# Gated cross-attention with RMS norm on one core: the setup's weight loads, transposes and first product rearranged

## The chip, the cores and the metric

The kernel runs on one core of a Trainium2 chip. The metric is the device time in microseconds of one execution, start to end. The kernel before was run three times: 1008.8, 1011.82 and 1014.79 us, median 1011.82. A profile is one further execution with the hardware profiler on.

## What is computed

All tensors are float32. x is (8, 1024, 1024), the memory ctx is (8, 64, 512), W_mem is (1024, 512), W_gate is (1024, 2048), b_gate and norm_w have 1024 elements.

```
memory_proj    = ctx @ W_mem.T                             # (8, 64, 1024), "mp"
scores         = x @ memory_proj.T / sqrt(1024)            # (8, 1024, 64)
attn           = softmax(scores)
memory_context = attn @ memory_proj                        # (8, 1024, 1024)
gate           = sigmoid(concat(x, memory_context) @ W_gate.T + b_gate)
fused          = x + gate * memory_context
out            = fused * rsqrt(mean(fused**2) + 1e-6) * norm_w
```

W_gate falls into W1 (applied to x) and W2 (applied to memory_context). Since memory_context is attn @ mp, the kernel computes mp @ W2.T + b_gate once for all 512 memory rows ("G2") and applies attn to that; so only x @ W1.T is a large product. That one is done with Strassen-Winograd's seven products at two levels, hence the many sums and differences of quarters of x and of W1.

## The kernel before

The kernel is one long function with inner helpers. All of it is written out in program order (`pin` keeps each instruction in the order of the source, engine by engine). DMAs go out on SyncE's queue (helper `load`, L96), on ScalarE's queue (helper `scratch`, L99) and, for the residual, on GpSimd's. Dependences, and the completion semaphores of DMAs, are put in by the framework. TensorE's matmuls all come from the helper `mm` (L90), and two-operand sums from `tt` (L93), so in the profile they are told apart by their tiles.

Setup, L114 to L430:

- SyncE loads the memory (mem_sb, 4 DMAs of 128 rows), W_mem transposed (wm, 4 DMAs of 512 KB), the bias (broadcast to 128 partitions), the first half of the columns of W2 (w, 16 DMAs of 128 KB, runs of 2 KB), then W1 (ws, 32 DMAs of 128 KB, runs of 1 KB). Rows of W1 and W2 are loaded in quarters of 32 partitions (`rows_by_chunk`, L104), because the main loop transposes x in 32x32 blocks and the feature order must agree.
- TensorE transposes the memory through PSUM (pt_mem, L165), VectorE copies it out (memT, L171) and puts W_mem's columns into block order (wmp, L179).
- pm (L195 to L204): for each of eight blocks j of 128 features, four matmuls over the chunks k of the memory's 512 columns give mp transposed (mpT). ScalarE and VectorE copy the sums out by turns; pairs of blocks are stored to DRAM (mpd), from which the main loop loads each batch's part for the scores (mpb).
- TensorE transposes mpT back (pt_mp, L211), ScalarE copies it (L213) into `mp` and stores it to DRAM (mgd, L221), the rows that attn multiplies.
- pg (L400 to L428): eight sums n, for two halves h of W2's columns and four blocks q of 128 memory rows, each of eight 128x512 matmuls. VectorE adds the bias into a staging tile, ScalarE stores that to the other half of mgd. Between the adds VectorE works off `w1_tasks`: four large outer differences (128x2048) and 28 inner ones (128x512) of W1's blocks, which have a tile of their own for each of the seven outer products (`ws`, 7 slots each). After add 0 come the loads of W2's second half and of the first tile of x; after add 6 the block transposes of x, the first sums, and GpSimd's inner sums.

Main loop: sixteen tiles of 512 rows of x, seven outer products each, 49 products per tile. A table of due times (`plan`) puts loads, transposes, softmax, sums, sigmoid, residual and norm into fixed slots between the products. The first product of the first tile is kA of `outer_product` (L633).

The pools matter for the order: the xq pool has 4 buffers of 4 KB per partition (wm, then mp, then x), the gate pool 7 (W2, then the outputs), apool, rot and small one or two for each name; PSUM has five banks for sums in turn, two for the context and one for scores.

Of the kernel before, what the change touches and what calls it, by code (L numbers as in the profile page):

```python
# [8 lines left out]
F32 = mybir.dt.float32  # L9
AF = mybir.ActivationFunctionType  # L10
ALU = mybir.AluOpType
# [4 lines left out]
P = 128  # L16
# [4 lines left out]
def tile_gated_cross_attention_rmsnorm(  # L21
# [40 lines left out]
    nc = tc.nc  # L62
    B, N, D = x.shape
    M, E = mem.shape[1:]
# [3 lines left out]
    BM = B * M  # L68
    KD = D // P
    KE = E // P  # L70
    H = 512
    C = 256
    NPAIR = BM // P
# [15 lines left out]
    def mm(o, lhsT, rhs, start, stop):  # L89
        pin(nc.tensor.matmul(o, lhsT, rhs, start=start, stop=stop, skip_group_check=True))  # L90

    def tt(eng, o, a, b, op):
        pin(eng.tensor_tensor(o, a, b, op))  # L93

    def load(o, i):
        pin(nc.sync.dma_start(o, i))  # L96

    def scratch(o, i):
        pin(nc.scalar.dma_start(o, i))  # L99

    def t4k(pool, shape, tag, name):
        return pool.tile(shape, F32, tag=tag, name=name)
# [7 lines left out]
    def bank(n, shape, name):  # L110
        return ps.tile(shape, F32, tag=banks[n % 5], name=name)


    memr = mem.rearrange("b m e -> (b m) e").rearrange("(q p) e -> p q e", p=P)  # L114
    mem_sb = [t4k(rot, [P, 2, E], "l2", f"mem_sb{i}") for i in range(2)]
    for q in range(NPAIR):
        load(mem_sb[q // 2][:, q % 2, :], memr[:, q, :])
    wm = []
    for k in range(KE):
        t = t4k(xqpool, [P, D], "xq", f"wm{k}")  # L120
        load(t, w_mem_t[k * P : (k + 1) * P, :])
        wm.append(t)
    bias_sb = t4k(small, [P, D], "junk", "bias_sb")
    load(bias_sb, b_gate.partition_broadcast(P))
    w2r = rows_by_chunk(w_gate_t[D:, :])
    w2 = {}

    def load_w2(h):
        for k in range(KD // 2):
            t = t4k(gpool, [P, 2, H], "gate", f"w2_{k}_{h}")  # L130
            for i in range(4):
                load(
                    t[32 * i : 32 * (i + 1), :, :],
                    w2r[i][:, 2 * k : 2 * k + 2, h * H : (h + 1) * H],
                )
            w2[k, h] = t

    load_w2(0)

    w1r = rows_by_chunk(w_gate_t[:D, :])  # L140
    ws = {o: const.tile([P, 7, 2, C], F32, name=f"ws{o}") for o in range(1, 8)}
    R11, R21, R12, R22, T4, T1, T2 = range(7)
    for o, k, h in ((1, 0, 0), (7, 0, 1), (3, 1, 1), (2, 1, 0)):
        for i in range(4):
            for n in range(2):
                load(
                    ws[o][32 * i : 32 * (i + 1), 2 * n : 2 * n + 2, :, :],
                    w1r[i][:, 4 * k : 4 * k + 4, h * H + n * C : h * H + (n + 1) * C],
                )
    nw_sb = const.tile([P, D], F32, name="nw_sb")  # L150

    ident = const.tile([P, P], F32, name="ident")
# [3 lines left out]


    mpd = dram.tile([P, KD, BM], F32, name="mpd")
    mgd = dram.tile([B, 2, M, D], F32, name="mgd")
    memT = [t4k(apool, [P, 2, BM], f"a1{i + 1}", f"memT{i}") for i in range(2)]  # L160
    for q in range(NPAIR):
        pt = bank(q, [P, KE, P], f"pt_mem{q}")
        for k in range(KE):
            pin(
                nc.tensor.transpose(  # L165
                    pt[:, k, :], mem_sb[q // 2][:, q % 2, k * P : (k + 1) * P], ident
                )
            )
        for i in range(2):
            pin(  # L170
                nc.vector.tensor_copy(  # L171
                    memT[i][:, :, q * P : (q + 1) * P], pt[:, 2 * i : 2 * i + 2, :]
                )
            )
    wmp = []
    for k, tag in enumerate(("a21", "a22", "s1", "s2")):
        t = t4k(apool, [P, KD, P], tag, f"wmp{k}")
        pin(
            nc.vector.tensor_copy(  # L179
                t.rearrange("p j (i r) -> p j i r", r=32),  # L180
                wm[k].rearrange("p (i j r) -> p j i r", i=4, r=32),
            )
        )
        wmp.append(t)

    mpT = [
        t4k(rot, [P, 2, BM], tag, f"mpT_{tag}_{i}")
# [4 lines left out]
    def mp_rows(j, q):  # L192
        return mpT[j // 2][:, j % 2, q * P : (q + 1) * P]

    for j in range(KD):  # L195
        pm = bank(j, [P, BM], f"pm{j}")
        for k in range(KE):
            mm(pm, wmp[k][:, j, :], memT[k // 2][:, k % 2, :], k == 0, k == KE - 1)
        dst = mpT[j // 2][:, j % 2, :]
        if j % 2 == 0:  # L200
            pin(nc.scalar.copy(dst, pm))
        else:
            pin(nc.vector.tensor_copy(dst, pm))
            scratch(mpd[:, j - 1 : j + 1, :], mpT[j // 2])  # L204

    for q in range(NPAIR):
        stage = t4k(xqpool, [P, D], "xq", f"mp{q}")
        for h in range(2):
            pt = bank(2 * q + h, [P, 4, P], f"pt_mp{q}_{h}")
            for j in range(4):  # L210
                pin(nc.tensor.transpose(pt[:, j, :], mp_rows(4 * h + j, q), ident))  # L211
            pin(
                nc.scalar.copy(  # L213
                    stage.rearrange("p (i j r) -> p j i r", i=4, r=32)[
                        :, 4 * h : 4 * h + 4, :, :
                    ],
                    pt.rearrange("p j (i r) -> p j i r", r=32),
                )
            )
        for i in range(2):  # L220
            scratch(mgd[2 * q + i, 0], stage[i * M : (i + 1) * M, :])  # L221


    def outer_sum(o, a, b):
        tt(nc.vector, ws[o][:, 0:4, :, :], ws[a][:, 0:4, :, :], ws[b][:, 0:4, :, :], ALU.subtract)

    def inner_sums(o):
        w = ws[o]
        for s, a, b in ((T1, R12, R11), (T2, R22, T1), (R12, R22, R12), (T4, R21, T2)):
            yield lambda s=s, a=a, b=b: tt(  # L230
                nc.vector, w[:, s, :, :], w[:, a, :, :], w[:, b, :, :], ALU.subtract
            )


# [2 lines left out]
        *inner_sums(1),  # L237
        lambda: outer_sum(6, 3, 5),
        lambda: outer_sum(7, 3, 7),
        lambda: outer_sum(4, 2, 6),  # L240
    ] + [f for o in (6, 7, 5, 4, 2, 3) for f in inner_sums(o)]


    xq, A, S, L2, O = {}, {}, {}, {}, {}
# [59 lines left out]
    def inner_s(q, o, part):  # L304
        l11, l12, l21, l22 = quarters(left(q, o))
        if part == 0:
            L2[q, o] = t4k(rot, [P, 4, 2, P], "l2", f"l2_{q}_{o}")
        s1, s2, s3, s4 = (L2[q, o][:, i, :, :] for i in range(4))
        if part == 0:
            tt(nc.gpsimd, s1, l21, l22, ALU.add)  # L310
            tt(nc.gpsimd, s2, s1, l11, ALU.subtract)
        else:
            tt(nc.gpsimd, s3, l11, l21, ALU.subtract)
            tt(nc.gpsimd, s4, l12, s2, ALU.subtract)
# [71 lines left out]

    def load_mg(b):
        mgs[b] = t4k(small, [P, D], "mg", f"mg{b}")
        load(mgs[b], mgd[b].rearrange("g m d -> (g m) d"))


    first = [
# [7 lines left out]
    for h in range(2):  # L400
        cols = slice(h * H, (h + 1) * H)
        for q in range(NPAIR):
            pg = bank(n, [P, H], f"pg2_{h}_{q}")
            for k in range(KD):
                mm(pg, mp_rows(k, q), w2[k // 2, h][:, k % 2, :], k == 0, k == KD - 1)
            pool, tag = ((apool, "s4"), (small, "attnT"))[n % 2]
            stage = t4k(pool, [P, H], tag, f"g2_{h}_{q}")
            tt(nc.vector, stage, pg, bias_sb[:, cols], ALU.add)
            for i in range(2):
                scratch(mgd[2 * q + i, 1][:, cols], stage[i * M : (i + 1) * M, :])  # L410
            if n == 0:
                load_w2(1)
                for t in (0, 1, 2, 3):
                    load_xq(0, t)
                load(nw_sb, norm_w.partition_broadcast(P))
            if n < 6:
                while done < len(w1_tasks) * (n + 1) // 6:
                    w1_tasks[done]()
                    done += 1
            elif n == 6:  # L420
                for f in first:
                    f()
                for part in range(2):
                    inner_s(0, 1, part)
            n += 1
    load_mp(0)
    load_mg(0)
# [148 lines left out]
    def outer_product(q, o, ext):  # L576
# [1 line left out]
        nonlocal slot, banks  # L578
        l11, l12, l21, l22 = quarters(left(q, o))
        s1, s2, s3, s4 = (L2[q, o][:, i, :, :] for i in range(4))  # L580
        w = ws[o]
        kb = {}

        def product(name, tag, lhsT, s, start=True):
            nonlocal slot
            step()
            if name not in kb:
                kb[name] = ps.tile([P, C], F32, tag=banks[tag], name=f"k{name}{q}_{o}")
            for k in range(2):
                mm(kb[name], lhsT[:, k, :], w[:, s, k, :], start and k == 0, k == 1)  # L590
            slot += 1

        def o_blocks(row, h):
# [160 lines left out]
```

## Time and profile before

| What | Value |
|---|---|
| Three runs | 1008.8, 1011.82, 1014.79 us |
| Profiled execution | 1009.18 us, its span 1007.4 us |
| First product kA starts | 105.83 us into the span |
| pm on TensorE | 9.04 to 37.6 us |
| pg on TensorE | 44.56 to 105.8 us |
| A matmul of 128x512 | 0.43 us start to start |
| VectorE: 128x2048 difference, 128x512 difference, bias add | 2.29, 0.62, 0.69 us |
| SyncE: one DMA of 128 KB | issued in 0.35 to 0.47 us, landed after 2.4 us or more |
| HBM read and written | 85.98 and 39.85 MB |

How to read the lines below: "PE" is TensorE, "PEld" its weight loads, "DVE" VectorE, "ACT" ScalarE, "POOL" GpSimd, "SPq" and "ACTq" the DMA issues on the queues of SyncE and ScalarE. A line of the timeline has the start, the time taken, the engine, the source line, the operation, what it writes and reads by the program's tile names, the shape, how often, and in brackets how long the engine was idle before and what ended that. A line of stages has the stretch, its width, then busy time and count for PE, PEld, DVE, ACT and POOL, the granted TensorE clock, the share of DMA engines busy, and GB/s. A line of waits has who waited for whom, the total in us, the times, and the longest.

### The profile page before, as it was taken

Reading aid. Unit: us, or ns where it says so; the run is one execution under the profiler, and the core shown is the slowest. Engines: PE = TensorE matmul, PEld = TensorE weight load, DVE = VectorE, ACT = ScalarE, POOL = GpSimd, SP = SyncE. Lnnn points to the kernel's source line nnn. Section 1 sums busy time; section 2 is a strip of 40 time slices with the busy share of each in tenths; the row PEclk is TensorE's granted clock in tenths of the full one; section 3 lists DMA queues with packets and bytes.
Section 4 is the critical chain, followed back from the end, with each engine's and each line's share of the span. In section 5 each row is a group of like instructions: output and inputs, shape, how many; then the busy total and the mean of one; then the engine's idle time right before and its main releaser. Section 6 shows DMA issues by size and latency. Waiting matters only on the chain.

```text
span 1007.4 us, 14639 instructions
## 1 busy us (share of the span) xinstructions
PE 978.7 (97%) x4976; PEld 765.6 (76%) x4976; DVE 760.2 (75%) x1478; ACT 324.7 (32%) x600; POOL 688.0 (68%) x851
## 2 busy tenths in 40 slices
PE   7898999999999999999999999999999999999995
PEld 3443688888878887888888788878888887888883
DVE  2075667878878787878788787878787887878777
ACT  0200023334241523333342415233333424152344
POOL 0000577878878687878788786878787887868772
PEclk9999999999999999999999999999999999999998
DMA  8676508263633727182715546181826363372512
GB/s 255 198 182 180 135 1 178 84 138 97 157 101 84 188 78 164 63 185 87 163 60 130 141 104 158 52 199 63 178 83 137 96 167 97 84 188 89 142 63 84
DMA packets 76522, 126.79 MB, mean 126 GB/s; under 512 B 16288, under 2 KB 53152, under 8 KB 76448
## 3 DMA queue, kind: packets, MB, share of 16 engines
q1 hardware_dynamic: 65312, 88.11, 30.1%
q0 software_dynamic: 8640, 31.46, 17.0%
q10 hardware_dynamic: 2496, 6.29, 2.1%
q8 instruction: 39, 0.64, 0.3%
q14 instruction: 35, 0.29, 0.1%
HBM read 85.98 MB, written 39.85 MB: 125 GB/s over the span
## 4 chain that ended last, share of the span: by engine, by line
PE 79%; DVE 14%; DMA 3%; issue 2%; SPq 1%; ACT 1%; ACTq 0%; POOL 0%; DVEq 0%
PE kA L90 16%; PE pc L90 11%; PE kE L90 9%; PE kF L90 8%; PE kD L90 8%; PE kB L90 8%; PE kC L90 7%; PE psT L90 6%; DVE gate L520 4%; DVE gate L93 3%; PE pm L90 2%; PE pg L90 2%; DVE e L93 2%; DVE u L93 1%; DMA mgd<-g 1%
## 5 line engine op out<-in xcount | busy, mean ns | idle before, releaser
L93 POOL TENSOR_TENSOR gate<-gate,u 128x256 f32<-128x256 f32 x336 | 269.2, 831 | 122.3 <-DVE u L93 100.8
L93 POOL TENSOR_TENSOR l<-a 128x256 f32<-128x256 f32 x128 | 125.6, 981 | 163.3 <-DVE a L267 100.0
L491 ACT ACTIVATE gate<-gate 128x512 f32<-128x512 f32 x128 | 79.1, 629 | 397.7 <-DVE gate L93 397.6
L90 PE MATMUL kA<-ws,a 128*128 128x256 f32 x512 | 131.7, 380 | 0.4 <-ACT u L634 0.4
L90 PE MATMUL pc<-mg,attnT 64*128 64x256 f32 x512 | 127.4, 389 | 0.0
L520 DVE SCALAR_TENSOR_TENSOR gate<-gate,ss,nw_sb 128x512 f32<-128x512 f32 x120 | 116.5, 980 | 1.1
L90 PE MATMUL kC<-ws,l 128*128 128x256 f32 x448 | 115.1, 379 | 0.8 <-DVE g L93 0.8
L90 PE MATMUL kD<-ws,l 128*128 128x256 f32 x448 | 115.0, 379 | 0.0
L90 PE MATMUL kB<-ws,l 128*128 128x256 f32 x448 | 115.0, 379 | 0.0
L90 PE MATMUL kF<-ws,l 128*128 128x256 f32 x448 | 115.0, 379 | 0.0
L90 PEld LDWEIGHTS pc<-mg,attnT 64*128 64x128 f32 x512 | 90.6, 186 | 29.7 <-issue 21.2
L90 PEld LDWEIGHTS kA<-ws,a 128*128 128x128 f32 x512 | 97.0, 190 | 14.7 <-ACT u L634 1.2
L90 PE MATMUL kA<-ws,s 128*128 128x256 f32 x384 | 100.3, 384 | 1.1 <-ACT u L634 1.1
L90 PEld LDWEIGHTS kB<-ws,l 128*128 128x128 f32 x448 | 85.1, 190 | 11.6
L90 PEld LDWEIGHTS kF<-ws,l 128*128 128x128 f32 x448 | 85.1, 190 | 11.6
L90 PEld LDWEIGHTS kC<-ws,l 128*128 128x128 f32 x448 | 83.8, 190 | 11.8 <-POOL l L93 1.1
L90 PEld LDWEIGHTS kD<-ws,l 128*128 128x128 f32 x448 | 83.9, 190 | 10.7
L93 DVE TENSOR_TENSOR gate<-gate,pc 128x512 f32<-128x512 f32 x128 | 87.1, 680 | 5.5 <-ACT gate L491 5.5
L267 DVE STREAM_TRANSPOSE a<-xq 128x512 f32<-128x512 f32 x128 | 86.0, 693 | 0.0
L90 PEld LDWEIGHTS kA<-ws,s 128*128 128x128 f32 x384 | 71.6, 190 | 16.7 <-DVE a L93 6.2
L93 POOL TENSOR_TENSOR l<-s 128x256 f32<-128x256 f32 x96 | 77.9, 811 | 8.0 <-PE kF L90 5.4
L93 DVE TENSOR_TENSOR u<-u,kB 128x256 f32<-128x256 f32 x112 | 46.8, 418 | 46.2 <-PE kB L90 40.2
(94 smaller groups left out, 1695.4 us busy)
## 6 DMA issues: line engine op xcount, KB each, us to landing
xq<-in_x SPq DMA_DIRECT2D x256, 128.0 KB, 5.5
gate<-in_x POOLq DMA_DIRECT2D x60, 512.0 KB, 7.5
out<-gate SPq DMA_DIRECT2D x60, 512.0 KB, 2.6
w<-in_w_gate_t SPq DMA_DIRECT2D x32, 128.0 KB, 3.4
ws<-in_w_gate_t SPq DMA_DIRECT2D x32, 128.0 KB, 3.1
mg<-mgd SPq DMA_DIRECT2D x8, 512.0 KB, 3.6
wm<-in_w_mem_t SPq DMA_DIRECT2D x4, 512.0 KB, 6.4
mgd<-mp ACTq DMA_DIRECT2D x8, 256.0 KB, 4.4
```

Source lines behind the costliest of these rows:

```text
L90: pin(nc.tensor.matmul(o, lhsT, rhs, start=start, stop=stop, skip_group_check=True))
L93: pin(eng.tensor_tensor(o, a, b, op))
L267: nc.vector.transpose(A[key][:, :, r * P : (r + 1) * P].rearrange("p j (s c) -> p s j c", c=32), xq[q, t].rearrange("p s (j r) -> p s j r" ...
L491: pin(nc.scalar.activation(g, g, AF.Sigmoid))
L520: nc.vector.scalar_tensor_tensor(g[:, cols], g[:, cols], rstd[:, t % 2 : t % 2 + 1], nw_sb[:, cols], ALU.mult, ALU.mult,)
```

## The change

- Loads: the memory comes in eight DMAs of 128 KB (two halves of 256 rows, each in four quarters of the columns, runs of 512 B) into block layout `memq`, W_mem in sixteen DMAs of 32 whole rows; in the order first half of the memory, first chunk of W_mem, second half, other chunks. W2 comes as eight tiles of whole rows (32 DMAs of 32 rows of 4 KB), all ahead of W1; W1 as two tiles of whole rows (32 DMAs), no longer as quarters in the tiles `ws`. What used to be slots of `ws` is now a view of these tiles, of three tiles for outer differences, or a slot of a small tile `it` (`w_op`).
- Transposes: the memory and mp are transposed by VectorE in 32x32 blocks (4 and 16 instructions of 128x512), not by TensorE. The copies of the pm sums are all on VectorE.
- pm: the chunks k are the outer loop and the eight sums are open together in eight PSUM banks; the first chunk is done in two halves of the columns.
- Stores: mpd's four stores follow all eight copies in the source; mp's rows go to mgd in sixteen DMAs of 128 KB in place of eight of 256 KB; the bias adds' results in eight of 256 KB in place of sixteen.
- pg: as before, with whole-row tiles; the staging tiles are those of mg and attnT. The W1 differences are spread over five adds in place of six, in another order; the first tile's transposes follow adds 5 and 6.
- mg is loaded in two DMAs.

The diff, cut to its core:

```diff
-    memr = mem.rearrange("b m e -> (b m) e").rearrange("(q p) e -> p q e", p=P)
-    mem_sb = [t4k(rot, [P, 2, E], "l2", f"mem_sb{i}") for i in range(2)]
-    for q in range(NPAIR):
-        load(mem_sb[q // 2][:, q % 2, :], memr[:, q, :])
-    wm = []
-    for k in range(KE):
-        t = t4k(xqpool, [P, D], "xq", f"wm{k}")
-        load(t, w_mem_t[k * P : (k + 1) * P, :])
-        wm.append(t)
+    memq = [t4k(rot, [P, BM // 64, E // 4], "l2", f"memq{i}") for i in range(2)]
+    wm = [t4k(xqpool, [P, D], "xq", f"wm{k}") for k in range(KE)]
+    def load_mem(g):
+        for i in range(4):
+            load(memq[g][32 * i : 32 * (i + 1), :, :], memr[g, i])
+    def load_wm(k):
+        for i in range(4):
+            load(wm[k][32 * i : 32 * (i + 1), :], wmr[i, k])
+    load_mem(0)
+    load_wm(0)
+    load_mem(1)
+    for k in range(1, KE):
+        load_wm(k)
...
-    load_w2(0)
+    for k in range(KD):
+        t = t4k(*((gpool, [P, D], "gate") if k < 7 else (apool, [P, D], "s4")), f"w2_{k}")
+        for i in range(4):
+            load(t[32 * i : 32 * (i + 1), :], w2r[i][:, k, :])
+        w2.append(t)
...
+    w1 = [const.tile([P, 4, D], F32, name=f"w1_{h}") for h in range(2)]
+    for h in range(2):
+        for k in range(4):
             for i in range(4):
+                load(w1[h][32 * i : 32 * (i + 1), k, :], w1r[i][:, 4 * h + k, :])
...
+    def w_op(o, s):
+        if s >= T4:
+            return inner_t[o][:, s - T4, :, :]
+        k, n = {R11: (0, 0), R21: (1, 0), R12: (0, 1), R22: (1, 1)}[s]
+        return outer_b[o][:, 2 * k : 2 * k + 2, n * C : (n + 1) * C]
...
+    transpose_mem(0, 0)
+    order_wm(0)
+    transpose_mem(1, 0)
+    order_wm(1)
+    transpose_mem(0, 1)
+    transpose_mem(1, 1)
+    order_wm(2)
+    order_wm(3)
...
+    for k in range(KE):
+        for cols in ([slice(0, BM // 2), slice(BM // 2, BM)] if k == 0 else [slice(0, BM)]):
+            for j in range(KD):
+                mm(
+                    pm[j][:, cols],
+                    wmp[k][:, j, :],
+                    memT[k // 2][:, k % 2, cols],
+                    k == 0 and cols.start == 0,
+                    k == KE - 1,
+                )
     for j in range(KD):
-        pm = bank(j, [P, BM], f"pm{j}")
-        for k in range(KE):
-            mm(pm, wmp[k][:, j, :], memT[k // 2][:, k % 2, :], k == 0, k == KE - 1)
...
+        pin(nc.vector.tensor_copy(mpT[j // 2][:, j % 2, :], pm[j]))
+    for j in range(0, KD, 2):
+        src = mpT[j // 2]
+        load2(mpd[:, j : j + 2, :], src)
+        for g in range(4):
             pin(
+                nc.vector.transpose(
+                    mpq[g].rearrange("p s (j r) -> p s j r", r=32)[:, :, j : j + 2, :],
+                    src[:, :, g * P : (g + 1) * P].rearrange("p j (s c) -> p s j c", c=32),
                 )
             )
+    for g in range(4):
+        for i in range(4):
+            load2(
+                mgd[0, g * P : (g + 1) * P, i * Q4 : (i + 1) * Q4].rearrange(
+                    "(s c) e -> c s e", c=32
+                ),
+                mpq[g][32 * i : 32 * (i + 1), :, :],
+            )
...
-                mm(pg, mp_rows(k, q), w2[k // 2, h][:, k % 2, :], k == 0, k == KD - 1)
-            pool, tag = ((apool, "s4"), (small, "attnT"))[n % 2]
-            stage = t4k(pool, [P, H], tag, f"g2_{h}_{q}")
+                mm(pg, mp_rows(k, q), w2[k][:, cols], k == 0, k == KD - 1)
+            stage = t4k(small, [P, H], ("mg", "attnT")[n % 2], f"g2_{h}_{q}")
             tt(nc.vector, stage, pg, bias_sb[:, cols], ALU.add)
-            for i in range(2):
-                scratch(mgd[2 * q + i, 1][:, cols], stage[i * M : (i + 1) * M, :])
+            load2(mgd[1, q * P : (q + 1) * P, cols], stage)
             if n == 0:
-                load_w2(1)
                 for t in (0, 1, 2, 3):
                     load_xq(0, t)
                 load(nw_sb, norm_w.partition_broadcast(P))
-            if n < 6:
-                while done < len(w1_tasks) * (n + 1) // 6:
+            if n < 5:
+                while done < len(w1_tasks) * (n + 1) // 5:
                     w1_tasks[done]()
                     done += 1
-            elif n == 6:
-                for f in first:
+            elif n == 5:
+                for f in first[:6]:
                     f()
                 for part in range(2):
                     inner_s(0, 1, part)
+            elif n == 6:
+                for f in first[6:]:
+                    f()
```

`load2` is the helper `scratch` under another name.

## Prediction

> **What bounds the kernel now.** I read the page first, then the busy times by stage, the chain of waits, the timeline of the first 125 us, and what SyncE's queue (SP) waited for.
>
> ```profile
> PE 978.7 (97%) x4976; PEld 765.6 (76%) x4976; DVE 760.2 (75%) x1478; ACT 324.7 (32%) x600; POOL 688.0 (68%) x851
> ...
> PE 79%; DVE 14%; DMA 3%; issue 2%; SPq 1%; ACT 1%; ACTq 0%; POOL 0%; DVEq 0%
> ```
>
> ```profile
> 0.00:40.00 40.00, 34.32 (x102) 17.29 (x103) 8.37 (x16) 4.70 (x7) 0.74 (x7) 1.00 0.70 218
> 40.00:104.00 64.00, 56.96 (x137) 25.17 (x136) 35.23 (x46) 3.22 (x6) 2.63 (x4) 0.97 0.72 192
> ...
> 170.00:292.00 122.00, 121.41 (x654) 99.02 (x648) 98.63 (x195) 43.23 (x79) 94.80 (x115) 1.00 0.49 120
> ```
>
> The second fence is the busy time by stage: PE's is the first number after the width. From 170 us on TensorE has no gap (121.41 of 122), so the main loop is TensorE's own work and the change does not touch its count. The setup, up to the first product kA at 105.83 us, has gaps. Hence one question: when does the first product start, and is it then held up?
>
> The work that TensorE must do before that is small. A 128x512 matmul runs at 0.43 us start to start (58 of them in 25.17 us, chain of waits). The pm product has 64 of them, 27.4 us; the pg product has 128, 54.9 us: 82.3 of 105.8 us. The other 23.5 us are transposes, waits and a slow clock:
>
> ```profile
> 3.75 3.74 PE L165 MATMUL pt_mem<-ident,mem_sb 128*128 128x128 f32 x16 [3.75 <-DMA mem_sb<-in_mem]
> ...
> 44.56 5.40 PE L90 MATMUL pg<-w,mpT_l 128*128 128x512 f32 x8 [2.14 <-ACT mp L213]
> ...
> 83.44 1.96 PE L90 MATMUL pg<-w,mpT_u 128*128 128x512 f32 x4 [2.34 <-DMA w<-in_w_gate_t]
> ```
>
> pm ends at 37.6, the mp transposes and ScalarE's copies keep pg until 44.56, the first eight pg matmuls take 5.40 us instead of 3.6, and the second half of W2 arrives late twice (1.69 and 2.34 us).
>
> Then the queues, which decide this case:
>
> ```profile
> SPq L96 <- DMA mgd<-g: 29.4, 10, 5.0
> SPq L96 <- DMA mpd<-mpT_u: 9.6, 1, 9.6
> SPq L96 <- DMA mpd<-mpT_l: 8.1, 2, 4.5
> ```
>
> ```profile
> 17.81 0.35 ACTq L99 DMA_DIRECT2D mpd<-mpT_l  x1
> ...
> 21.05 1.72 SPq L96 DMA_DIRECT2D w<-in_w_gate_t  x4
> ...
> 41.04 24.48 SPq L96 DMA_DIRECT2D ws<-in_w_gate_t  x24
> ```
>
> A weight load on SP waits for a store of ScalarE's queue to land, though it reads nothing of it. The built program says why: the DMAs of both queues take eight completion semaphores in one common turn, and each waits for the DMA that last had its semaphore. The 22nd load has the semaphore of the first mpd store, issued at 17.81 and landed 3.2 us later; SP resumes at 21.05. So a load placed a turn behind a store cannot start before the store has.
>
> **What the Trainium skill says.** "DMA: Bandwidth & Descriptors", section "Anatomy of one DMA — SWDGE (gpsimd) path": DMA engines do not wait on semaphores; any wait happens on the issuing sequencer ahead of dispatch. So one blocked load blocks all behind it; the 9.6 us above agree. "TensorE: Matmul & The Clock Gate", Part 1: an idle TensorE falls to half clock and needs a busy window of about 3.4 us to leave it. The trace agrees: weight loads of pg are 0.86 us apart from 44.56 to 48.05, then 0.43. "VectorE: DVE Perf Modes", section "The three transpose paths": VectorE transposes independent 32x32 blocks, hence the loads in quarters. The trace's stream transposes of 128x512 come 6 in 3.67 us.
>
> **The change, part by part.** Times are on the span's clock.
>
> *Start.* Eight 128 KB loads (mem's first half, W_mem's first chunk) go out at 0.47 us each, as the wm loads do (2.60 to 4.68 for four), so the last at 4.0. Small loads land in 2.5 to 2.9 us, so about 6.8; the reorder is 0.69: TensorE starts at 7.6, not at 9.04 (its transposes were at 3.75). Chunks outermost lets it run on: each later chunk is needed 6.9 us after the last, and four loads are issued in 1.9 us. But TensorE is now cold at 7.6; half clock for 3.4 to 6.8 us costs 1.7 to 3.4, I take 2.2. pm ends at 7.6+27.4+2.2 = 37.2. Before, 37.6: taking 16 transposes off gains 0.4 only. (The first chunk in two halves adds matmuls of 256, 0.215 us each as in kA, but no columns.)
>
> *Transposes of mp.* 32 TensorE transposes and 8 ScalarE copies between pm and pg go (44.56-37.6 = 7 us, plus 1.7 of cold clock). pg can start at once if W2 is there. The 16 VectorE transposes (16 x 0.61 = 9.8 us) stand behind the eight pm copies, which end 0.9 us after pm: from 38.1 to 47.9. They hide beside pg; the bias adds queued behind them have five banks.
>
> *The loads.* In the new order the stores are fewer semaphores away. W2's first seven loads go ahead of everything. The eighth (last quarter of chunk 1) has the semaphore of mpd's first store, the tenth, eleventh and twelfth those of the other three. With chunks outermost all eight sums end together: sum j ends at 37.2-(7-j)x0.86, its copy 0.9 later, so mpd's stores go at 33.0, 34.7, 36.4, 38.1 (before: the first at 17.81). They land 2.6 us later, as the one at 38.41 with nothing beside it. So SP stands still from about 15 us, where the seven loads are out, to 35.6. Four semaphores then pass to the 16 mgd stores, four serve SP; 13 more loads go in fours, a landing (2.5) apart: 41, 43.5, 46, 48.5. The second quarter of chunk 6 waits for the 13th mgd store.
>
> *The stores.* The first four are released by the 13th transpose, 38.1+13x0.61 = 46.1. Each group of four has the semaphores of the group before, so it is four landings in a row. A 128 KB store lands in 2.3 (nothing beside it, 61 us) to 3.3 us; ScalarE needs about 2.0 to issue four. I take 2.45 for a round: the 13th has landed at 46.1+9.8 = 55.9. Six loads at 0.47 put the last W2 load at 58.7, landing 2.4 later: 61.1.
>
> *pg.* The first sum takes its chunks as they come and ends at 61.1+1.7 (two cold matmuls) = 62.8. Seven more at 6.86 are 48.0; the rest of the cold clock 0 to 1.7, I take 0.9. pg ends at 111.7 instead of 105.83: +5.9. Before, kC then stood 0.75 for VectorE's add; this does not come on top if VectorE is in time.
>
> *VectorE.* Its first add (63.7) releases a store that lands at about 66.3, and a W1 load waits for that store; 21 loads remain, 9.9 us, plus 2.6 to land: W1 is complete at 78.6. From there VectorE has 3 large sums (6.6), 24 inner sums (14.9), adds 1 to 6 (3.7), eight transposes (4.9) and two S sums (3.0): 33.1, then the last add, 112.4; kC wants it at 111.7+1.7 = 113.4. In time, by 1 us. The order of sums is moved, not added to. xq waits for the stores of adds 1 and 2 (landed about 90), and is needed at 103: hidden by 10 us. mpb is needed 7 us after kA; mg, which now shares its buffer with the staging of adds 0, 2, 4 and 6 and so waits for the last of their stores, and the next xq behind it come about 4 us later against their users than before, with some 28 us to spare: nothing. The eight bias stores of 256 KB in place of sixteen of 128 save ScalarE issues that nobody waits for.
>
> *Sum.* +5.9-0.75 = +5.15, say 5.2 us. The profiled execution took 1009.18 (span 1007.4): 1014.4. The median of the runs shown is 1011.82, so I forecast 1017.0.
>
> Unknown costs, both ends: start and clock -1 to +1.7; store rounds 4 x (2.2 to 3.0), -1 to +2.2; loads at 2.2 to 3.0 us, -0.5 to +1; the rest of the cold clock -0.9 to +0.8; later steps on whole-row tiles in the main loop 0, since runs of 256 floats stay contiguous. Together some -3 to +5 on 1017.0.
>
> **Rivals.** (A) The semaphore turn does not bind, loads stream at 0.47 us: W2 is complete by 30 us, W1 by 45, pg starts at 37.2 and ends at 92.1. VectorE, from 47.9: 26.5 of w1 sums, 5.5 of adds, 7.9 for the first tile make 87.8, in time. That is faster by 13.7: 998. For it: 23 us of setup are not matmuls, and 4 KB packets take 0.16 us, 400 GB/s over 16 engines. Against: the SP waits above are this very wait, in the kernel before. It decides if the eighth W2 load is issued before 20 us. (B) It binds, but rounds and loads are quick (2.1 and 2.2 us) and the clock recovers at once: pg ends 108 to 110, 1012 to 1016, no measurable change. (C) VectorE becomes the bound: W1 is complete 3 us later (81.6), its row of 33.1 us ends at 115.4, and kC waits for it: 1019 to 1023. For it: the margin is 1 us and nothing in that row can be skipped; against: TensorE's own lateness usually moves with it.
>
> **How the numbers follow.** The forecast (1015 to 1020) 0.55, A 0.08, B 0.17, C 0.20. About 0.5% (5.06 us) is what a measurement can tell from no change. The forecast lies on that bound and is split: slower 0.30+0.20 = 0.50, same 0.25+0.17 = 0.42, faster 0.08. Range 1010 to 1024, with 2 to 3 us for the spread of the runs (1008.8 to 1014.79); it leaves out A and the tail of C.
>
> **What would show it.** SP idle from about 15 to 35 us for "mpd", again until about 56 for "mgd<-mpq"; mpd's first store at 33; TensorE waiting for w up to 61 us in the first pg; a half clock near 60; kA at 111 to 112; main loop at 121.4 of 122. Wrong, if W2 is complete before pm ends, or if VectorE's last add, not pg, is what kC waits for.

## The result, and the profile after

The changed kernel takes 1019.44 us (median of six runs, 1018.47 to 1019.9); the kernel before takes 1010.13 us (six runs, 1008.8 to 1014.79). The ratio is 1.0083, with a 95% interval of 1.0063 to 1.0104: 9.3 us slower by the medians. The profiled execution took 1018.77 us with a span of 1017.0, against 1009.18 and 1007.4. In the spans the loss is 9.6 us. One execution each of two versions below lasted far longer than its others (3587 and 1288 us); it is left out of their medians.

Engine totals and the chain that ended last, from the page of the kernel after:

```profile
PE 978.6 (96%) x4944; PEld 765.0 (75%) x4944; DVE 767.1 (75%) x1494; ACT 317.3 (31%) x588; POOL 687.3 (68%) x851
...
PE 82%; DVE 13%; DMA 2%; issue 1%; SPq 1%; ACT 0%; POOL 0%; ACTq 0%; DVEq 0%
```

TensorE's total is the same (978.6 against 978.7), so the loss is idle time, not work. The busy time by stages of the kernel after:

```profile
0.00:40.00 40.00, 31.85 (x83) 17.85 (x84) 11.50 (x18) 0.00 (x0) 0.73 (x7) 1.00 0.53 153
40.00:104.00 64.00, 51.53 (x105) 20.53 (x105) 29.84 (x46) 0.00 (x0) 0.00 (x0) 0.84 0.82 221
...
170.00:292.00 122.00, 121.63 (x660) 98.92 (x659) 96.45 (x191) 44.84 (x83) 93.73 (x115) 1.00 0.56 132
```

The main loop is as full as before (121.63 of 122 us). The DMA engines' busy share in the first 40 us fell from 0.70 to 0.53, although more loads were meant to go out early, and from 40 to 104 us TensorE's granted clock fell from 0.97 to 0.84. The queue of SyncE says why. Its main waits from 0 to 95 us, in us in all, times and longest:

```profile
SPq L96 <- DMA mpd<-mpT_l: 18.7, 2, 17.5
...
SPq L96 <- DMA mgd<-g: 6.7, 2, 3.8
...
SPq L96 <- DMA mgd<-mpq: 3.5, 1, 3.5
```

For 17.5 us on end no load is issued, because one of W2's loads waits for the first store of mpd. TensorE's timeline shows the effect:

```profile
7.91 30.80 PE L90 MATMUL pm<-memT,wmp 128*128 128x256 f32 x80 [7.91 <-DVE wmp L195]
...
45.99 2.04 PE L90 MATMUL pg<-w,mpT_l 128*128 128x512 f32 x2 [5.09 <-DMA w<-in_w_gate_t]
...
65.36 3.60 PE L90 MATMUL pg<-w,mpT_l 128*128 128x512 f32 x8
...
113.42 1.03 PE L90 MATMUL kA<-w,a 128*128 128x256 f32 x4
...
117.48 1.10 PE L90 MATMUL kC<-w,l 128*128 128x256 f32 x4 [2.17 <-DVE g L93]
```

Each matmul of the source stands as two records (pg has 64 in the source and 128 records), so an x2 is one chunk k of a sum, and x8 is four. pg's first sum now starts at 38.55 instead of 44.56, but needs 27 us, as W2's eight tiles come one at a time. From the third chunk on, its two records take 2.04 us, at half speed, where eight records later take 3.60. The sums end at 113.42 instead of 105.83, and kC of the first product starts at 117.48 instead of 108.47 (+9.0). What kC waited for at the very end is VectorE's last bias add (the eight adds are numbered 0 to 7; 65.56 is add 0, 116.68 add 7):

```profile
65.56 0.69 DVE L93 TENSOR_TENSOR g<-pg,bias_sb 128x512 f32<-128x512 f32 x1 [20.87 <-PE pg L90]
...
84.19 2.29 DVE L93 TENSOR_TENSOR t<-w,t 128x2048 f32<-128x2048 f32 x1 [4.44 <-DMA xq<-in_x]
...
116.68 0.65 DVE L93 TENSOR_TENSOR g<-pg,bias_sb 128x512 f32<-128x512 f32 x1
```

The difference at 84.19 is the first that needs W1's second half. The releaser named, a load of x, is the one that came last by the profile's inference; this sum reads nothing of x. W1's last load was issued at 79.6 and landed at 83.9. From there VectorE has no gap up to 117.33.

### The profile page after: what moved, and what is told of

It reads as the page before. It is cut to its first block, busy times and chain, and to the rows that moved or that the text cites. A ratio compares the mean times of both kernels' runs of the same rounds, so it can differ in the third digit from the quotient of the medians.

```text
span 1017.0 us, 14611 instructions
## 1 busy us (share of the span) xinstructions
PE 978.6 (96%) x4944; PEld 765.0 (75%) x4944; DVE 767.1 (75%) x1494; ACT 317.3 (31%) x588; POOL 687.3 (68%) x851
## 4 chain that ended last, share of the span: by engine, by line
PE 82%; DVE 13%; DMA 2%; issue 1%; SPq 1%; ACT 0%; POOL 0%; ACTq 0%; DVEq 0%
PE kA L90 16%; PE pc L90 11%; PE kE L90 9%; PE kF L90 8%; PE kD L90 8%; PE kB L90 8%; PE kC L90 7%; PE psT L90 6%; PE pg L90 5%; DVE gate L556 4%; PE pm L90 3%; DVE gate L93 3%; DVE e L93 2%; DVE u L93 1%; DMA mgd<-mpq 1%
## 5 line engine op out<-in xcount | busy, mean ns | idle before, releaser
L90 PE MATMUL kD<-it,l 128*128 128x256 f32 x448 | 115.0, 379 | 0.0
L90 PE MATMUL kB<-it,l 128*128 128x256 f32 x448 | 115.0, 379 | 0.0
L90 PE MATMUL kA<-w,a 128*128 128x256 f32 x384 | 98.8, 380 | 0.4 <-ACT u L669 0.4
L90 PEld LDWEIGHTS kB<-it,l 128*128 128x128 f32 x448 | 85.1, 190 | 11.6
L90 PEld LDWEIGHTS kD<-it,l 128*128 128x128 f32 x448 | 83.9, 190 | 10.7
L90 PEld LDWEIGHTS kA<-w,a 128*128 128x128 f32 x384 | 72.8, 190 | 11.4 <-ACT u L669 1.2
L90 PE MATMUL kE<-it,a 128*128 128x256 f32 x256 | 69.0, 392 | 0.0
L90 PE MATMUL kC<-w,l 128*128 128x256 f32 x256 | 65.8, 379 | 2.2 <-DVE g L93 2.2
L90 PE MATMUL kA<-t,s 128*128 128x256 f32 x256 | 67.4, 386 | 0.0
L90 PE MATMUL kF<-w,l 128*128 128x256 f32 x256 | 65.7, 379 | 0.0
```

## The experiments

Each edit is on the kernel after unless it says otherwise. The kernel before, run beside each, had medians from 1009.8 to 1014.2 us with single runs from 1008.7 to 1014.9, so versions are compared by their own times and by the start of kC.

**The stores on GpSimd's queue.** This takes ScalarE's stores out of the turn of semaphores that the prediction speaks of.

```
 def load2(o, i):
-    pin(nc.scalar.dma_start(o, i))
+    pin(nc.gpsimd.dma_start(o, i))
```

> The changed kernel with all setup stores (mpd, mgd from mp's rows, mgd from the bias adds) issued on GpSimd's queue, whose DMAs have completion semaphores of their own. Theory (loads wait in turn behind stores that share their semaphores): SyncE never stands still before the loads of x, W2 is complete by about 34 us and W1 by about 52, pg runs from 38.6 to 93.5 without a gap, kC starts near 95.3 instead of 117.5, and the time is 997 (22 less than the changed kernel, 13 less than the kernel before). Rival (the loads of whole rows to 32 partitions are slow by themselves): the queue moves on, but W2 is still incomplete at 50 us, pg ends no earlier than 105, and the time is 1008 or more.

Measured: 995.34 us (three runs), ratio 0.9856 (0.9835 to 0.9877). The profile is from a second run of the same kernel.

> The kernel after with the twenty-eight stores of mp and of g issued from GpSimd's queue instead of ScalarE's, once more, for a profile. If the stores hold up SP's loads only through a semaphore that loads and stores take in turn: W2's and W1's 64 loads are issued one behind the other without a stand-still (0.55 us each, done by about 50 us), the sums of pg run from about 39 without a wait on W2 and end at about 93.5, kC of the first product starts at 95 to 96 and no longer waits on VectorE; time 995 to 997. If the loads were slow for lack of bandwidth and not for the turn: W2's last row lands near 60 as before, pg ends near 112, time near 1019.

Measured: 994.96 us, ratio 0.9845 (0.9817 to 0.9873). From the timelines of TensorE and of SyncE's queue:

```profile
37.22 3.60 PE L90 MATMUL pg<-w,mpT_l 128*128 128x512 f32 x8
...
92.15 1.03 PE L90 MATMUL kA<-w,a 128*128 128x256 f32 x4
...
93.88 1.03 PE L90 MATMUL kC<-w,l 128*128 128x256 f32 x4
```

```profile
13.10 39.13 SPq L96 DMA_DIRECT2D w<-in_w_gate_t  x64
```

All 64 weight loads go out in one run. pg is one block from 37.22 to 92.15 (the prediction's rival A had 37.2 to 92.1), and kC waits for nothing. The coupling of the queues thus costs the changed kernel 24.5 us (1019.44 - 994.96).

**The same edit in the kernel before** (its helper is called `scratch`).

> The kernel before with the same stores on GpSimd's queue. Theory: the wait exists there too, but is mostly covered: pg no longer waits for W2's second half (4.0 us less), ScalarE's copies between pm and pg no longer have store issues among them (about 2 us less), kC near 101.5 to 102 instead of 108.5, time about 1003.5. So of what the changed kernel gains without the coupling, about half is the change's own. Rival (the coupling costs the kernel before nothing, it only hurts the changed order): 1009 to 1011, no difference.

Measured: 1000.93 us, ratio 0.9911 (0.9891 to 0.993); kC starts at 98.75, earlier than expected. The coupling costs the kernel before 9.2 us (1010.1 - 1000.9). Without it the change gains 6.0 us (1000.9 - 995.0), most of it in the start of pg, 37.22 against 41.15: that is the transposes of mp taken off TensorE. So the change is good for 6 us and buys 15 us more of coupling: -6.0 + 24.5 - 9.2 = +9.3. The sum comes out by construction: it splits the measured 9.3 us and does not confirm them.

**The stores on SyncE's own queue, behind the loads** (`nc.scalar.dma_start` becomes `nc.sync.dma_start` in `load2`). The turn stays, but no load of W2 or W1 has a store ahead of it.

> The kernel after with all its stores issued on SP's own queue, behind the loads of W1 in program order, so that no load of W2 or W1 can wait for a store although the semaphores are still taken in one turn. If ScalarE's stores held up the loads by the turn: W1 is complete near 57 as with the stores on GpSimd, pg runs from about 37.5 without a wait to 92.5, and the time is 995 to 998 (the loads of x stand behind g's stores now and may come late for VectorE's transposes at 81: up to 1002). If it is the hardware queue of ScalarE against GpSimd's, for instance the landing of the stores, that matters: no better than half of it, over 1007.

Measured: 999.74 us, ratio 0.9897 (0.9869 to 0.9925). pg runs from 38.17 to 93.11 without a gap. So GpSimd's queue is not needed for the gain: what counts is which DMA stands ahead of which in the turn. The last 5 us against GpSimd's queue come with a new wait, VectorE's for a staging tile that a late store of g still reads:

```profile
DVE g L93 <- DMA mgd<-g: 10.4, 2, 5.4
```

```profile
99.50 2.04 PE L90 MATMUL kC<-w,l 128*128 128x256 f32 x4 [3.12 <-DVE g L93]
```

In the profiled execution (1002.8 us, above the median) kC starts 5.6 us later than with the stores on GpSimd's queue, and as TensorE then runs at half speed for a while (kC takes 2.04 us instead of 1.03), the scores behind the first product start 8.4 us later.

**Only mpd's four stores on GpSimd's queue.** This shifts the turn so that the long stand-still has another cause, and leaves the chain of mgd's stores.

```
-        load2(mpd[:, j : j + 2, :], src)
+        pin(nc.gpsimd.dma_start(mpd[:, j : j + 2, :], src))
```

> The kernel after with only the four stores of mpd issued from GpSimd's queue; the 24 stores of mgd stay on ScalarE's. In the turn of the eight semaphores, as the built program lists it, the loads of W2's rows 2 to 5 then fall between the stores without meeting one, and the first load that has to wait for a store is one of row 6, for the 13th store of mgd. If the turn is the mechanism: SP's stand-still at 17.5 us is gone, it comes later instead and lasts until the 13th store has landed (54 to 57.5, as four rounds of stores from 43.7 take 2.5 to 3.5 us each); W2 is complete near 59 to 62, W1 near 80 to 83; time 1014 to 1018, so the stand-still of 17.5 us that is gone buys 1 to 5 us. If the first stand-still itself were the loss: pg starts without waits as with all stores on GpSimd, time 997 to 1003. If neither: 1019.4.

Measured: 1014.57 us (17 runs), ratio 1.003 (1.0019 to 1.004); kC at 113.34. From SyncE's waits, its timeline and TensorE's:

```profile
SPq L96 <- DMA mgd<-mpq: 21.5, 1, 21.5
```

```profile
52.34 1.71 SPq L96 DMA_DIRECT2D w<-in_w_gate_t  x4
```

```profile
56.33 2.04 PE L90 MATMUL pg<-w,mpT_u 128*128 128x512 f32 x2 [12.64 <-DMA w<-in_w_gate_t]
```

The wait of 17.5 us is gone, and one of 21.5 us for another store has come. It lasted until the 13th store of mgd had landed, at 52.33, and SyncE went on at 52.34. So the first stand-still by itself wasn't the loss. What sets the end of W2 is the four rounds of stores of mgd, each waiting for the round before. The chain of waits has landings of them (start, us), first in the kernel after (the 2nd, 8th and 13th store, then W2's last load), then in this one (the 2nd, 6th, 10th and 14th store, one landing behind the other):

```profile
44.11 4.54 DMA mgd<-mpq
...
49.52 4.27 DMA mgd<-mpq
...
54.22 3.26 DMA mgd<-mpq
...
60.20 3.26 DMA w<-in_w_gate_t
```

```profile
43.97 2.46 DMA mgd<-mpq
46.45 2.06 DMA mgd<-mpq
...
50.66 2.53 DMA mgd<-mpq
```

With W2's loads standing still, these stores of 128 KB land in 2.06 to 2.53 us; with loads between them they took 3.26 to 4.54. The 13th landed at 52.33 instead of 57.48, W2's last load at 58.65 instead of 63.46, and VectorE's row behind W1 starts at 80.05 instead of 84.19. Of the 5.1 us at the 13th store, 4.1 reach kC.

**pm with its blocks outermost again**, the one part of the change undone that sets when mpd's stores can start.

```
-    for k in range(KE):
-        for cols in (...):
-            for j in range(KD):
...
+    for j in range(KD):
+        for k in range(KE):
+            mm(pm[j], wmp[k][:, j, :], memT[k // 2][:, k % 2, :], k == 0, k == KE - 1)
```

> The changed kernel with one part undone: pm has the blocks j outermost again and the chunks k inside, so it starts when all four chunks are in order (16.5 us instead of 7.9), but its sums end one by one and mpd's stores go out from about 27.6, 7 us apart, instead of from 34.3. Theory (when the stores go out decides, not when pm starts): pm ends at 47, yet W2 is complete at about 57 instead of 63.5, because its last loads now have the semaphores of stores that have gone; pg ends near 105.5; W1 is complete near 82 behind the last mgd stores, VectorE is the bound, kC at 115 and the time 1017. Rival (pm's end carries through): pm is 8 us later, so is everything, 1027.

Measured: 1014.61 us, ratio 1.0044 (1.0028 to 1.006). pm starts later (10.95 instead of 7.91) and ends later, and pg still ends 14 us earlier than after, near 99, since the first store of mpd goes at 23.95 instead of 34.32 and W2's first sum is through at 51.2. But:

```profile
104.79 2.08 PE L90 MATMUL kA<-w,a 128*128 128x256 f32 x4 [5.38 <-DVE a L294]
...
112.64 2.04 PE L90 MATMUL kC<-w,l 128*128 128x256 f32 x4 [2.17 <-DVE g L93]
```

TensorE's sums are through 14 us earlier and kC starts only 4.8 us earlier: W1 was complete at 79.36, and VectorE's row behind it ended 33.1 us later, at 112.49. In the kernel after the same row took 33.1 us from 84.19. So with TensorE out of the way the end is the landing of W1 plus this row. The start of pm (expected at 16.5), the end of pg (expected at 105.5) and kC all came earlier than expected. kA now waits for VectorE too, and after these waits TensorE runs the first product at half speed (kC takes 2.04 us): in the profiled execution (1016.67 us, above the median) only 2.1 of kC's 4.8 us are left in the span (1014.9 against 1017.0).

**VectorE's row made shorter.** First by giving eight of its inner sums to GpSimd:

```
-                nc.vector, w_op(o, s), w_op(o, a), w_op(o, b), ALU.subtract
+                nc.gpsimd if o in (2, 3) else nc.vector,
+                w_op(o, s), w_op(o, a), w_op(o, b), ALU.subtract
```

> The changed kernel with the 8 inner W1 differences of outer products 2 and 3 on GpSimd instead of VectorE; the queues are as they were. Theory (VectorE's row from W1's last load to add 7 is what kC waits for last, 2.2 us behind pg): the row is 5 us shorter, pg still ends at 113.4, kC starts at 115.2 instead of 117.5, time 1017.1. Rival (the chain through W2's last load and pg is the only one): kC and the time stay, 1019.4.

Measured: 1020.57 us, ratio 1.0106 (1.0083 to 1.0129); kC at 118.95, still waiting for add 7. The experiment did not take the load off: VectorE's own sums slowed down beside GpSimd's (VectorE's timeline, then GpSimd's).

```profile
97.89 0.68 DVE L93 TENSOR_TENSOR it<-t 128x512 f32<-128x512 f32 x1
98.61 1.64 DVE L93 TENSOR_TENSOR it<-t,it 128x512 f32<-128x512 f32 x1
100.17 1.75 DVE L93 TENSOR_TENSOR t<-t 128x512 f32<-128x512 f32 x1
101.84 0.68 DVE L93 TENSOR_TENSOR g<-pg,bias_sb 128x512 f32<-128x512 f32 x1
```

```profile
98.05 1.65 POOL L93 TENSOR_TENSOR w<-w 128x512 f32<-128x512 f32 x1 [10.09 <-DVE t L93]
...
101.33 1.71 POOL L93 TENSOR_TENSOR it<-w 128x512 f32<-128x512 f32 x1
```

The Trainium skill, "SBUF — State Buffer", section "SBUF: two separate sides", says that a VectorE operation with two SBUF inputs and a GpSimd operation that reads SBUF exclude each other for the whole instruction. The trace agrees: 1.64 and 1.75 us in place of 0.68 where both inputs lie in SBUF, and 0.68 for the bias add at 101.84, one input of which lies in PSUM, although GpSimd reads SBUF all the while (101.33 to 103.04).

Then by moving the same eight sums out of the setup into free slots of the first tile:

```
-        *(f for o in (6, 4, 2, 3) for f in inner_sums(o)),
+        *(f for o in (6, 4) for f in inner_sums(o)),
...
+    for i, f in enumerate(f for o in (2, 3) for f in inner_sums(o)):
+        at(10 + 2 * i, f)
```

> The kernel after with the eight inner sums of the products 2 and 3 (each some 0.65 us on VectorE) taken out of the setup and put into slots 10 to 24 of the first tile, where these products are still ahead. If VectorE's row behind W1's last load is what ends last: the row is 5.2 us shorter, kC starts at 112.3 to 113, unless the sums of pg (end 113.4) or the landing of g's stores now end last, which keeps it at 115.2; time 1014.5 to 1017.2. If VectorE's row is not the bound: kC stays at 117.5 and the time at 1019.4. If VectorE has no room in the first tile, some of it comes back there: over 1019.4.

Measured: 1018.29 us, ratio 1.0073 (1.0047 to 1.0099). Its VectorE and TensorE timelines:

```profile
115.58 0.69 DVE L93 TENSOR_TENSOR g<-pg,bias_sb 128x512 f32<-128x512 f32 x1 [0.41 <-PE pg L90]
```

```profile
117.11 1.03 PE L90 MATMUL kC<-w,l 128*128 128x256 f32 x4
```

VectorE's last add now waits for pg, and kC for nobody: VectorE's row was the last in the kernel after. But kC starts only 0.4 us earlier, because in this execution W2 came later, half clock lasted into the second sum, and pg ended at 115.38 instead of 113.42. The interval of the time overlaps with that of the kernel after, so the time alone tells nothing. Two limits lie some 2 us apart, and taking one away shows the other.

**W1 in runs of 1 KB again**, with the same 32 loads of 128 KB.

```
-        for k in range(4):
+        for c in range(4):
             for i in range(4):
-                load(w1[h][32 * i : 32 * (i + 1), k, :], w1r[i][:, 4 * h + k, :])
+                load(
+                    w1[h][32 * i : 32 * (i + 1), :, c * C : (c + 1) * C],
+                    w1r[i][:, 4 * h : 4 * h + 4, c * C : (c + 1) * C],
+                )
```

> The kernel after with W1 loaded in runs of 1 KB (the same 32 loads of 128 KB, each 32 partitions by 4 rows by 256 columns), everything else alike: the part of the change that makes rows whole, undone. If the kind of run matters as the queue of the kernel before with its stores on GpSimd showed it (0.735 us a load of 1 KB runs against 0.55 for whole rows): W1 is complete 2 to 4 us later than 84.2, and kC and the time with it: 1021 to 1023. If only the turn of the semaphore sets when W1 lands: 84.2 and 1019.4 again.

Measured: 1019.68 us (three runs), ratio 1.0091 (1.0057 to 1.0125), not to be told apart from the kernel after. The difference that needs W1's second half starts at 85.93 instead of 84.19, and 1.5 us of that are add 0 coming later. Whole rows of W1 neither gain nor lose here, where the loads behind add 0's store are issued 0.47 us apart either way.

**TensorE's clock ahead of pm.** On the kernel with the stores on GpSimd's queue, since pm's end is not hidden there: transposes of the identity into a PSUM tile that nobody reads, 16 of them and then 28.

```
     make_identity(nc, ident)
+    hot = ps.tile([P, BM], F32, tag="sc", name="hot")
+    for _ in range(16):
+        pin(nc.tensor.transpose(hot[:, :P], ident, ident))
```

> The kernel with the stores on GpSimd's queue, and sixteen transposes of the identity on TensorE (into a PSUM tile that nobody reads) ahead of the first product of W_mem, so that its clock has risen when they start at 7.9 us. If the 3.3 us that the product lost to the cold clock lie on the path: it ends at about 35.4 instead of 38.7, pg's sums start 3 us earlier and the time is 992 to 993 against 995.5. If W2's loads (last issued at 47.9, first half needed from 36) then come too late for pg, the gain goes into waits of pg on W2: 994.5 to 996.

Measured: 995.96 us. The sixteen were done by 5.04, and pm was as slow as in the kernel after:

```profile
1.36 3.68 PE L174 MATMUL hot<-ident 128*128 128x128 f32 x16 [1.36 <-POOL ident masks.py:199]
8.22 30.73 PE L90 MATMUL pm<-memT,wmp 128*128 128x256 f32 x80 [3.19 <-DVE wmp L198]
```

> As the kernel with sixteen transposes of the identity ahead, but with 28 of them: at 0.23 us each they fill TensorE from 1.4 to 7.8 us, where the sixteen left it idle from 5.0 to 8.2. If the product of W_mem loses 1.8 to 3.3 us because its clock is not up, and what brings it up is unbroken work just before: it takes 27.5 us instead of 29.3 to 30.8, ends at 35.5 to 35.7, and the time is 992.5 to 994 against 995.0. If the start of the clock does not follow from work ahead: 29.3 to 30.8 again, time 995 to 996.

Measured: 995.01 us, so no gain in time, though pm did what was expected:

```profile
8.10 27.77 PE L90 MATMUL pm<-memT,wmp 128*128 128x256 f32 x80 [0.80 <-DVE wmp L198]
...
94.03 1.10 PE L90 MATMUL kC<-w,l 128*128 128x256 f32 x4 [1.50 <-DVE g L93]
```

pm takes 27.77 us instead of 29.29, and kC waits 1.50 us for VectorE: it starts at 94.03, where it started at 93.88 without the transposes. The 28 differ from the sixteen both in their length and in the gap behind them, and which of the two counts was not separated.

**All three together**: stores on GpSimd's queue, 28 transposes, the eight sums in the first tile.

> Three edits on the kernel after together: the stores on GpSimd's queue, 28 transposes of the identity ahead, and the eight inner sums of the products 2 and 3 moved into the slots of the first tile. With the first two alone VectorE held up kC by 1.5 us (it started at 94.0). If that wait is what took the clock's gain: kC starts at 92.3 to 92.6 without a wait on VectorE and the time is 993 to 994. If the eight sums are in the way in the first tile (VectorE's last product sums come later there), or another wait takes over: 995 again.

Measured: 993.64 us (993.4 to 993.97), ratio 0.9802 (0.9786 to 0.9818). pm again takes 27.77 us, and kC starts at 92.41 without a wait. So the clock's gain had gone to VectorE's row. This is the fastest version here, 25.8 us below the kernel after, and 1.3 of these come from the last two edits.

## Why the prediction was right, and where its steps failed

The forecast was 1017.0 us in a range of 1010 to 1024; 1019.44 lies inside, on the slower side. By the prediction's own sign ("Wrong, if ... VectorE's last add, not pg, is what kC waits for") its main line failed at the end: what came is its rival C, to which it gave 0.20, and the range held because it covered most of C. The mechanism that both share, loads of weights that wait for stores by the common turn of semaphores, is shown by the runs: two ways of taking it away give 995.0 and 999.7 us, and moving its place keeps half of the loss (4.4 of 9.3 us) and most of what the coupling costs (19.6 of 24.5). Part of the closeness of the absolute number is luck: the predicted difference was 5.2 us and the measured one 9.3. It was hung on 1011.82, the median of the three runs shown; on the 1010.13 of six runs it would have given 1015.3.

- *Start and clock of pm*: 7.6 predicted, 7.91 measured. The cold clock was taken at 2.2 us and cost 3.3 (pm 30.80 us against 27.4), so pm ended 1.5 us later than the 37.2 predicted. The granted clock of the table of stages reads 1.00 here and does not show this; the records do, with some 3.6 matmuls a us up to 14 us and 6 a us behind it. The Trainium skill, "TensorE: Matmul & The Clock Gate", Part 1, adds that the window runs freely and that the cold stretch therefore varies; the runs agree that it varies: 29.29 to 30.83 us for a pm without work right before it, 27.77 with it.
- *Stand-still of SyncE's queue*: predicted from about 15 to 35.6, measured from 19.5 to 37.0. The end is late by pm's clock. It began later because W2's sixth and seventh load waited for other loads first, the longest time (2.4 us) for the bias; that cost nothing.
- *Transposes of mp on VectorE*: mis-sized. They are 128x256, not the 128x512 that the working and the description of the change took, and cost 0.34 us each (eight in 2.72), not 0.61. The first store of mgd went at 43.74 instead of 46.1: 2.4 us to the good, in spite of the late end of pm.
- *Rounds of stores*: mis-sized the other way. 2.45 us for a round came from stores with little beside them; with W2's loads between them a landing took 3.26 to 4.54. The 13th store landed at 57.5 instead of 55.9, the last load of W2 at 63.46 instead of 61.1 (3.26 us on the way instead of 2.4). The experiment with mpd's stores on GpSimd's queue points to the loads beside them: with the loads standing still the stores took 2.06 to 2.53 us.
- *pg*: first sum over at 65.4 instead of 62.8, end at 113.42 instead of 111.7. The half clock ended with the first sum, so the 0.9 us taken for its rest did not come.
- *VectorE "in time, by 1 us"*: this is the step that failed. The length of its row was about right (33.1 us with the last add, 84.19 to 117.33, where 33.1 and 0.7 for the last add were taken), its start wrong: the row could begin at 84.19, not 78.6. Of the 5.6 us, 1.9 are add 0, which came later; about 1.8 are add 0's store, which let SyncE go on at 69.95 where 66.3 was predicted; and about 2 the last load, issued at 79.6, 4.3 us on the way instead of 2.6, with 0.3 more until VectorE began. The issue of the loads between took 9.7 us, as taken. So kC waited for VectorE, which is rival C: it named 3 us of lateness and 1019 to 1023.
- *The sum*: kC would have started 1.7 us after the end of pg, at 115.2, by the forecast's own chain; VectorE added 2.3 us. The experiment with the eight sums moved to the first tile showed that the forecast's chain stands close behind: with VectorE out of the way pg ended 2 us later in that execution, and that decided.
- *Rival A* said 998 us if the turn does not bind, and what must be seen for it. It binds, and with it taken out 995.0 was measured, with pg where the rival had it; the loads took 0.61 us each ((51.6 - 13.1) / 63), not 0.47, and that was still early enough.
- *Main loop*: predicted at nothing, and the stretch from 170 us is unchanged. kC accounts for 9.0 of the 9.6 us of span; the remaining 0.6 was not traced.

Whether loads of 32 partitions are slower per byte than larger ones was not tried, apart from W1's length of run, and stays open.

## What to carry to other kernels

When two queues draw their completion semaphores from one small pool in a common turn, the place of a DMA in program order couples it to DMAs with which it shares no data: before loads are moved ahead of stores, list who has whose semaphore, and price the stand-still of the whole queue behind it. Put stores that wait for late results on a queue outside that turn, or behind the last load that matters; here that was worth more (9 and 24 us) than the rearrangement itself (6 us). And a row of work on another engine that is in time by 1 us is not in time: price the landing of its last input with the traffic that will be there, not from a quiet stretch.

## What the runs showed of the hardware that was not expected

- The stores of 128 KB in the chain of waits took 3.26 to 4.54 us to land with loads between the stores and 2.06 to 2.53 us with the loads standing still, on the same queue in the same program position.
- A wait of TensorE cost more than its length: after waiting 3.12 us for VectorE (stores on SyncE's queue) kC took 2.04 us instead of 1.03, and a lateness of 5.6 us at kC was one of 8.4 us at the scores.
- Sixteen transposes that ended 3.2 us before pm left its clock as cold as none (30.73 us); 28 that ended 0.8 us before it, and in the last version 1.5 us, saved nearly the whole cold stretch (27.77 us both times, of which 27.4 are the matmuls at full clock).
- VectorE's 128x512 differences went from 0.68 to 1.64 to 1.75 us beside GpSimd's of the same size, which took 1.60 to 1.71 themselves there and 1.26 with VectorE idle: giving eight of the 28 inner sums to GpSimd gained nothing.
